# Two graph layers on one core: the second layer's input turned by VectorE from DRAM blocks, with features in another order

## The chip, the cores and the metric

The kernel runs on one core of a Trainium2 chip. Time is device microseconds of that core for one launch. Three runs of the kernel before gave a median of 1999.9 us (1999.46 to 2000.22).

## What is computed

x holds 128 graphs of 128 nodes with 256 features, adj 128 matrices of 128 x 128. Everything is 32-bit float. Two layers follow each other, each with a residual and a layer norm:

```
# layer 0
f_hom = adj @ ((x @ theta) * norm) * norm          # norm = (row sum of adj)^-0.5
f_het = x @ W_h
gate  = sigmoid(x @ W_t + b_t)
x1    = layernorm(x + elu(gate * f_hom + (1 - gate) * f_het))
# layer 1, on x1
h     = relu(bn1(conv1(x1)))                       # 1 tap, along the nodes
x_conv= relu(bn2(conv2(h)) + x1)                   # 17 taps along the nodes, 256 -> 256
s     = x1 @ w_se + b_se;  A = exp(-|s_n - s_m|^2) # node to node
x_nmp = A @ relu(x1 @ w_msg + b_msg)
out   = layernorm(x1 + GRU([x_conv, x_nmp], x1))
```

## The kernel before

The kernel has three stages, each with its own pools. P is 128 (partitions, nodes), D is 256 (features), NC = 2 halves of the features, J = 2 graphs in a pair, NP = 64 pairs.

**Stage A** (lines 541 to 643) runs over the pairs in rounds. A round of `a_round(t)` works on several pairs at once: TensorE projects pair t (`l0_project`, lines 343 and 348), VectorE and ScalarE finish layer 0 of pair t-1 (`l0_gate`, `l0_elu`, `l0_norm`), and layer 1 of pair t-2 and t-3 is begun: `l1_turn` makes x1 feature-major, `l1_front` multiplies it by conv1 (line 413), `l1_analyse` takes h to Fourier coefficients H (line 433). A product over features wants them on the partitions, while x1 comes out with nodes there. `transposed` (line 302) does this turn with four TensorE transposes (line 307) into a PSUM bank and one VectorE copy (line 311). x itself is turned in another way: `load` (line 117) reads it in 32-row blocks, so that the 32 x 32 block transpose of VectorE (line 317) completes the turn, without TensorE.

`l1_store` writes x1 (line 425) and its turned form x1T (line 426) to DRAM for stage C. `w_unit` (line 444) takes one group of conv2's taps to Fourier coefficients in every second round, at the end of the round (line 449, copied out by ScalarE at line 453 into four tiles), and `w_store` writes the four tiles in the next round (line 458). `v_unit` does the same for the eight leftover coefficients, in 19 of the other rounds (lines 480 and 484).

For rounds 3 to 63 the order is the one written in the code on TensorE, SyncE, VectorE and ScalarE; for rounds -1 to 2 it is on TensorE alone, and a scheduler orders the others. All DMAs of stage A but a few at the start and the end are issued by SyncE (SP), in the order: x1 store, x1T store, x, the x blocks of pair t+2 (four transfers), adj, then the tap store, the next tap load (four transfers), and the leftovers'. The program's DMA completion semaphores are eight, used in turn, so that the issue of a DMA waits until the one eight places before it has landed.

PSUM has eight banks in stage A, used in turn (`bank`, line 112). VectorE's order in a round is: turn of x1, three operations of `l0_gate`, a wait for ScalarE's exp, `l0_elu` with the layer norm's statistics, the gate's bias (line 355), the norm's shift (line 292, which waits for GpSimd), the shift of conv1 (line 417), the turn of x for the next pair, the row sum of adj, and the mix (line 374).

**The tail** (lines 614 to 642) finishes the last pairs and computes four groups' messages early, from x1T read back (`m_load`, line 499).

**Stage B** (lines 740 to 772) multiplies the coefficients H by those of the taps, 68 steps with 512 KB of taps each (line 743), while the gate weights are loaded on ScalarE's queue (`gate_weights`, line 704). **Stage C** reads x1T and x1 back, and computes the rest of layer 1.

Of the kernel before, what the change touches and what calls it, by code (L numbers as in the profile page):

```python
# [14 lines left out]
P = 128  # L15
# [19 lines left out]
def gnn_layers_kernel(ctx: ExitStack, tc: tile.TileContext, a: dict, out: bass.AP):  # L35
# [24 lines left out]
    x1_d = dtile([NP, P, J * D], "x1_d")  # L60
    x1T_d = dtile([NP, P, NC, J * P], "x1T_d")
    w_d = dtile([M // 2, P, 2, NC, D], "w_d")
# [9 lines left out]
    ones = const.tile([P, P], F32, tag="ones", name="ones")  # L72
    nc.gpsimd.memset(ones, 1.0)
# [37 lines left out]

    def bank(name):
        return ps.tile([P, 512], F32, tag="ps", name=name)
# [3 lines left out]
    def load(p):  # L117
        s = st[p] = {}

        xb = s["xb"] = io.tile([P, J * Q, 2 * K], F32, tag="xb", bufs=2, name=f"xb_{p}")  # L120
        for q in range(Q):
            nc.sync.dma_start(
                xb[q * K : (q + 1) * K],
                x[p * J : (p + 1) * J, :, 2 * K * q : 2 * K * (q + 1)].rearrange(
                    "b (r i) d -> i (b r) d", i=K
                ),
            )
        s["adjT"] = io.tile([P, J, P], F32, tag="adjT", bufs=3, name=f"adjT_{p}")
        nc.sync.dma_start(s["adjT"], adjT[:, p * J : (p + 1) * J, :])
# [14 lines left out]


    load(0)
    for j, name in enumerate(("L0_gnn_theta", "L0_gnn_W_h", "L0_gnn_W_t")):

        v = a[name].rearrange("(q c i) e -> c q i e", q=Q, c=NC)
        for c in range(NC):  # L150
            (nc.sync if j == 2 else nc.scalar).dma_start(w0[:, c, j * D : (j + 1) * D], v[c])
# [11 lines left out]
    vec = setup.tile([8 * NC, P], F32, tag="vec", name="vec")  # L163
    for i, q in enumerate("vmgb"):
        for k in range(2):
            r = (2 * i + k) * NC
            nc.scalar.dma_start(
                vec[r : r + NC], a[f"L1_gnn_bn{k + 1}_{q}"].rearrange("(c p) -> c p", p=P)
            )

    load(1)
    nc.sync.dma_start(conv1_w[:, :, 0:D], a["conv1_wT"].rearrange("(c p) e -> p c e", p=P))
    nc.sync.dma_start(conv1_w[:, :, D:], a["w_seT"].rearrange("(c p) e -> p c e", p=P))
# [61 lines left out]
    def batch_norms():  # L235
        n = 2 * NC
        tv = bank("vec_ps")
        nc.tensor.transpose(tv[:, 0 : 4 * n], vec, ident[0 : 4 * n, 0 : 4 * n])
        col = setup.tile([P, 4 * n], F32, tag="col", name="col")
        nc.vector.tensor_copy(col, tv[:, 0 : 4 * n])  # L240
        inv_sqrt(scale, col[:, 0:n], BN_EPS, n)
        nc.vector.tensor_mul(scale, scale, col[:, 2 * n : 3 * n])
        nc.vector.tensor_mul(shift, col[:, n : 2 * n], scale)
        nc.vector.tensor_sub(shift, col[:, 3 * n : 4 * n], shift)

        yield
        diag = setup.tile([P, n, P], F32, tag="diag", name="diag")
        for i, v in enumerate((scale, shift)):
            for c in range(NC):
                nc.vector.tensor_scalar(diag[:, NC * i + c, :], ident, v[:, c : c + 1], None, ALU.mult)  # L250
        tr = bank("row_ps")
        nc.tensor.matmul(tr, lhsT=ones, rhs=diag.rearrange("p a b -> p (a b)"), start=True, stop=True)
        nc.vector.tensor_copy(shift1, tr[:, D : 2 * D])
        for c in range(NC):
            nc.vector.tensor_mul(conv1_w[:, c, 0:D], conv1_w[:, c, 0:D], tr[:, 0:D])
# [46 lines left out]
    def transposed(src, dst, name):  # L302

        t = bank(f"{name}_ps")
        for c in range(NC):
            for j in range(J):
                nc.tensor.transpose(  # L307
                    t[:, (c * J + j) * P : (c * J + j + 1) * P],
                    src[:, j, c * P : (c + 1) * P], ident,
                )  # L310
        nc.vector.tensor_copy(dst.rearrange("p c n -> p (c n)"), t)


    def l0_turn(p):
        s = st[p]
        s["xT"] = wf.tile([P, NC, J * P], F32, tag="xT", name=f"xT_{p}")
        nc.vector.transpose(  # L317
            s["xT"].rearrange("p c (b i) -> p c b i", i=K),
            s["xb"].rearrange("p b (c i) -> p c b i", c=NC),
        )  # L320
        adj = bank(f"adj_ps_{p}")
        for j in range(J):
            nc.tensor.transpose(adj[:, nodes(j)], s["adjT"][:, j, :], ident)  # L323
        norm = s["norm"] = small.tile([P, J], F32, tag="norm", name=f"norm_{p}")
        nc.vector.reduce_sum(
            norm, adj[:, 0 : J * P].rearrange("p (j n) -> p j n", j=J), axis=mybir.AxisListType.X
        )
        inv_sqrt(norm, norm, DEG_EPS, J)
# [72 lines left out]

    def l1_turn(p):
        s = st[p]
        s["x1T"] = wk.tile([P, NC, J * P], F32, tag="x1T", bufs=2, name=f"x1T_{p}")
        transposed(s["x1"], s["x1T"], f"x1T_{p}")
# [17 lines left out]
    def l1_store(p, queue=nc.sync):  # L423
        s = st[p]
        queue.dma_start(x1_d[p], s["x1"].rearrange("p j e -> p (j e)"))
        queue.dma_start(x1T_d[p], s["x1T"])
# [17 lines left out]
    def w_unit(u):  # L444
        t = wt[u % NW].rearrange("p i o -> p (i o)")
        pq = [bank(f"w_ps_{u}_{r}") for r in range(4)]
        for r in range(4):
            k = slice(32 * r, 32 * r + TAPS)
            nc.tensor.matmul(pq[r], lhsT=T[k, 0:P], rhs=t[k, :], start=True, stop=True)  # L449
        wo = s_w[u] = []  # L450
        for r in range(4):
            o = taps.tile([P, 2, D], F32, tag="wo", bufs=4, name=f"w_o_{u}_{r}")
            nc.scalar.activation(o.rearrange("p i o -> p (i o)"), pq[r], AF.Copy)  # L453
            wo.append(o)

    def w_store(u):
        for r, o in enumerate(s_w.pop(u)):
            nc.sync.dma_start(
                w_d[0 : P // 2, r * QF + u].rearrange("k r c o -> k r (c o)"),
                o.rearrange("p c o -> p (c o)"),  # L460
            )
# [16 lines left out]
    def v_unit(v):  # L478
        pl = bank(f"wl_ps_{v}")
        nc.tensor.matmul(  # L480
            pl, lhsT=TL, rhs=vt.rearrange("p c o -> p (c o)"), start=True, stop=True
# [4 lines left out]
    def v_store(v):  # L486
# [3 lines left out]
        for r in range(2):  # L490
            nc.sync.dma_start(
                w_d[P // 2 : M // 2, f : f + n, r].rearrange("k f c o -> f k (c o)"),
# [6 lines left out]
    def m_load(i):  # L499
        t = io.tile([P, J, D], F32, tag=("xb", "x")[i // 2], bufs=2, name=f"mx1T_{i}")  # L500
        t = t.rearrange("p j d -> p (j d)")
# [39 lines left out]
    def a_round(t):  # L541
# [5 lines left out]
        def between():  # L547
            on(t - 1, l0_gate)
            on(t - 3, l1_analyse)
# [4 lines left out]
        on(t - 2, l1_turn)  # L554
        l0_project(t, between, beside) if t >= 0 else between()
        on(t - 1, l0_norm)
        if t == 0:
            next(norms)
            l0_turn(1)
            table(AT2, (node, lag))  # L560

            cos, sin = T[:, 2:M:2], T[:, 3:M:2]
            both = setup.tile([P, M // 2 - 1], F32, tag="both", name="both")
            nc.vector.tensor_sub(both, sin, cos)
            nc.vector.scalar_tensor_tensor(sin, sin, -1.0, cos, ALU.mult, ALU.subtract)
            nc.vector.tensor_copy(cos, both)
        on(t - 2, l1_front)
        on(t - 2, l1_store)
# [21 lines left out]
        if t != 0:  # L590
            on(t + 1, l0_turn)
        if t == 3:
            nc.scalar.dma_start(w_msg, a["w_msgT"].rearrange("(c p) e -> p c e", p=P))
# [13 lines left out]
    for t in range(-1, 3):  # L607
        with tc.manual_schedule(engines={E.PE}):
            a_round(t)

    with tc.manual_schedule(engines={E.PE, E.SP, E.DVE, E.Activation}):
        for t in range(3, NP):
            a_round(t)
        last = NP - 1
        l0_gate(last)
        w_unit(units[last])
        l1_turn(last - 1)
        l1_analyse(last - 2)
        l0_elu(last)
        early = [m_project(0, "gate")]  # L620
        l1_front(last - 1)
        m_load(2)
        l1_store(last - 1)
        w_store(units[last])
        m_load(3)
        l0_norm(last)
        early.append(m_project(1, "het"))
# [4 lines left out]
        l1_turn(last)  # L632
        early = [m_project(2, "gate")]
        l1_front(last)
        early[0][0]()
        l1_analyse(last - 1)
# [3 lines left out]
        l1_store(last, nc.scalar)  # L640
# [26 lines left out]
    def others():  # L667
# [36 lines left out]
        def gate_weights(t, name, lo_n, lo_rz):  # L704
            for at, width, base in ((lo_rz, D, 0), (lo_n, P, 2 * D)):
                for h in range(2):
                    nc.scalar.dma_start(
                        t[:, :, h, at : at + width],
                        a[name][:, base + h * width : base + (h + 1) * width].rearrange(
                            "(c p) e -> p c e", p=P  # L710
                        ),
# [3 lines left out]
        yield from gate_weights(w_ih, "w_ihT", D, 0)  # L715
        yield from gate_weights(w_hh, "w_hhT", 0, P)
# [23 lines left out]
    with tc.manual_schedule(engines={E.Activation, E.Pool}):  # L740
        for k in range(M // 2):
            w = wb.tile([P, 2, NC, D], F32, tag="w", name=f"wb_{k}")
            nc.sync.dma_start(w, w_d[k])
# [64 lines left out]
    def load_x1(g):  # L808
        s = st[g]
        if g in EARLY:  # L810
# [8 lines left out]
            s["x1"].rearrange("p (r j) e -> p r (j e)", j=J),  # L819
            x1_d[2 * g : 2 * g + 2].rearrange("r n e -> n r e"),  # L820
# [302 lines left out]
```

## Time and profile before

| from the page and the trace's answers | value |
|---|---|
| the profiled execution | 1999.04 us, of which the span is 1997.1 us |
| TensorE's granted clock, mean over the span | 0.995 |
| DMA packets | 245115, 263.64 MB, mean 132 GB/s |
| busy in 100 to 200 us (stage A): PE, DVE, ACT, POOL | 100.00, 81.46, 62.90, 17.75 us |
| stage A's DMA share, 100 to 600 us by stretches | 0.62 to 0.64 |
| stage B's DMA share, 720 to 800 us | 0.97, 347 GB/s |
| first turn of x1 (line 311) starts; last one | 34.6 us; 678.2 us |
| first matmul of stage B (line 748) | 686.2 us |

The span runs from the first to the last instruction of the program on the core; some 2 us of the execution lie around it. A row of an instruction group gives its count, the union of its busy times, the mean duration of one in ns, and the idle time of its engine just before it with what ended it. A matmul's duration includes the way through the array, which the next one overlaps; what one costs in a full stream is the distance from its start to the next one's start.

### The profile page before, as it was taken

What the parts mean: (1) busy time and instruction counts of PE and PEld (TensorE: products, weight loads), DVE (VectorE), ACT (ScalarE), POOL (GpSimd) and SP (SyncE); (2) the same over time, 40 slices, a digit from 0 to 9 for tenths busy, and PEclk for the clock granted to TensorE, in tenths of its full rate; (3) what the DMA queues carried; (4) which work ended last, traced back from release to release, by engine and by line L of the source; (5) the groups of instructions that cost most, each with busy time, mean ns of one, the idle gap of its engine ahead of it and who ended that gap; (6) DMA issues with size and microseconds to landing.
All of it is one profiled execution on the core that took longest, in us unless ns stands there. A gap on an engine that the chain in (4) does not pass through costs nothing.

```text
span 1997.1 us, 26580 instructions
## 1 busy us (share of the span) xinstructions
PE 1971.5 (99%) x8451; PEld 1348.2 (68%) x8451; DVE 1448.3 (73%) x2866; ACT 747.0 (37%) x1489; POOL 630.3 (32%) x855
## 2 busy tenths in 40 slices
PE   7999999999999999999999999999999999999997
PEld 5666666666666788876666666666666666666664
DVE  6888888888888664467777777767777776776766
ACT  3666666666666511122222222323222232222222
POOL 1111111111111255544243333424323342433331
PEclk8999999999999999999999999999999999999999
DMA  4666666656565689972212212221221221221100
GB/s 119 200 188 201 186 198 187 206 182 206 177 200 182 237 319 332 316 250 91 70 58 81 71 58 65 81 65 64 81 60 64 70 81 51 78 76 39 46 22 21
DMA packets 245115, 263.64 MB, mean 132 GB/s; under 512 B 86143, under 2 KB 179825, under 8 KB 244977
## 3 DMA queue, kind: packets, MB, share of 16 engines
q1 hardware_dynamic: 238641, 256.17, 40.2%
q10 hardware_dynamic: 6336, 5.78, 1.0%
q8 instruction: 69, 1.13, 0.2%
q14 instruction: 69, 0.57, 0.1%
HBM read 157.01 MB, written 104.86 MB: 131 GB/s over the span
## 4 chain that ended last, share of the span: by engine, by line
PE 95%; DVE 2%; DMA 1%; ACT 0%; issue 0%; POOL 0%; SPq 0%; POOLq 0%; DVEq 0%; ACTq 0%
PE g_ps L1007 43%; PE f_ps L343 11%; PE conv_ps L413 5%; PE y_ps L748 5%; PE gate_ps L348 5%; PE msg_ps L884 5%; PE coef_ps L433 3%; PE nmp_ps L940 3%; PE conv_ps L848 3%; PE z_ps L761 3%; PE mix_ps L369 3%; PE x1T_ps L307 2%; PE w_ps L449 2%; PE conv_ps L855 1%; PE wl_ps L480 1%; PE adj_ps L323 1%
## 5 line engine op out<-in xcount | busy, mean ns | idle before, releaser
L343 PE MATMUL f_ps<-w,xT 128*128 128x512 f32 x512 | 243.7, 599 | 0.2 <-DVE xT L317 0.2
L177 POOL TENSOR_SCALAR rstd_b<-mv_b 128x2 f32<-128x2 f32 (+1 forms) x65 | 12.5, 192 | 529.6 <-DVE mv_b L285 529.6
L966 ACT ACTIVATE o<-o 128x1024 f32<-128x1024 f32 (+1 forms) x65 | 67.9, 1044 | 268.4 <-DVE o L1043 263.9
L1007 PE MATMUL g_ps<-t_h,sh 128*128 128x384 f32 x384 | 156.9, 490 | 0.0
L1007 PE MATMUL g_ps<-t_m,sm 128*128 128x384 f32 x384 | 155.3, 486 | 0.0
L1007 PE MATMUL g_ps<-t_c,sc 128*128 128x384 f32 x384 | 155.2, 486 | 0.0
L294 ACT ACTIVATE y<-y,nb_b,rstd_b 128x256 f32<-128x256 f32 x128 | 70.0, 593 | 219.1 <-DVE nb_b L292 219.1
L348 PEld LDWEIGHTS gate_ps<-w,xT 128*128 128x128 f32 x512 | 97.3, 190 | 70.9 <-issue 60.9
L177 POOL TENSOR_SCALAR rstd_a<-mv_a 128x2 f32<-128x2 f32 x64 | 12.3, 192 | 392.2 <-DVE mv_a L285 379.8
L348 PE MATMUL gate_ps<-w,xT 128*128 128x256 f32 x512 | 132.0, 380 | 1.4 <-DMA w<-in_L_gnn_W_t 1.4
L343 PEld LDWEIGHTS f_ps<-w,xT 128*128 128x128 f32 x512 | 88.8, 192 | 63.0 <-issue 61.8
L1040 POOL TENSOR_TENSOR u<-u,p 128x512 f32<-128x512 f32 x63 | 79.8, 1266 | 162.4 <-DVE p L1024 162.4
L748 PE MATMUL y_ps<-wb,H 128*128 128x256 f32 x544 | 128.5, 379 | 0.8 <-issue 0.8
L413 PE MATMUL conv_ps<-conv_w,x1T 128*128 128x259 f32 x512 | 122.5, 381 | 0.0
L756 POOL TENSOR_TENSOR ws<-wb 128x512 f32<-128x512 f32 x67 | 92.7, 1384 | 89.7 <-PE z_ps L761 55.4
L352 ACT ACTIVATE hom<-f_ps,norm 128x256 f32<-128x256 f32 x128 | 60.6, 473 | 157.5 <-PE f_ps L343 153.0
L748 PEld LDWEIGHTS y_ps<-wb,H 128*128 128x128 f32 x544 | 103.2, 190 | 15.2 <-POOL ws L756 1.0
L884 PE MATMUL msg_ps<-w_msg,cx1T 128*128 128x256 f32 x480 | 108.7, 379 | 0.0
L1007 PEld LDWEIGHTS g_ps<-t_c,sc 128*128 128x128 f32 x384 | 73.0, 190 | 50.9
L1007 PEld LDWEIGHTS g_ps<-t_m,sm 128*128 128x128 f32 x384 | 73.0, 190 | 50.9
L413 PEld LDWEIGHTS conv_ps<-conv_w,x1T 128*128 128x128 f32 x512 | 97.1, 190 | 14.6 <-ACT w_o L453 0.2
L1007 PE MATMUL g_ps<-w_hhT_w,cx1T 128*128 128x384 f32 x256 | 105.1, 492 | 0.0
(218 smaller groups left out, 4433.7 us busy)
## 6 DMA issues: line engine op xcount, KB each, us to landing
wb<-w_d SPq DMA_DIRECT2D x68, 512.0 KB
w_d<-w_o SPq DMA_DIRECT2D x128, 256.0 KB
y_d<-yb SPq DMA_DIRECT2D x68, 256.0 KB
xb<-in_x SPq DMA_DIRECT2D x256, 64.0 KB
x<-in_x SPq DMA_DIRECT2D x64, 256.0 KB
cx1T<-x1T_d SPq DMA_DIRECT2D x64, 256.0 KB
yt<-y_d SPq DMA_DIRECT2D x32, 512.0 KB
cx<-x_d SPq DMA_DIRECT2D x32, 512.0 KB
```

The source lines that it names most:

```text
L294: nc.scalar.activation(dst[:, q, :], src[:, q, :], AF.Identity, bias=nb[:, q : q + 1], scale=rstd[:, q : q + 1],)
L343: nc.tensor.matmul(pf, lhsT=xT[:, c, nodes(j)], rhs=w0[:, c, 0 : 2 * D], start=(c == 0), stop=(c == NC - 1),)
L348: nc.tensor.matmul(pg[:, j * D : (j + 1) * D], lhsT=xT[:, c, nodes(j)], rhs=w0[:, c, 2 * D : 3 * D], start=(c == 0), stop=(c == NC - 1),)
L352: nc.scalar.activation(hom[:, j, :], pf[:, 0:D], AF.Copy, scale=norm[:, j : j + 1])
L369: nc.tensor.matmul(pm[:, j * D : (j + 1) * D], lhsT=adjT_[:, j, :], rhs=hom[:, j, :], start=True, stop=True,)
L413: nc.tensor.matmul(ph[:, 0 : D + CO], lhsT=s["x1T"][:, c, nodes(j)], rhs=conv1_w[:, c, :], start=(c == 0), stop=(c == NC - 1),)
L748: nc.tensor.matmul(py[:, blk, :], lhsT=coefs(blk if k == 0 else 2 * k + 1 - blk, c), rhs=w[:, blk, c, :], start=(c == 0), stop=(c == NC - 1),)
L756: nc.gpsimd.tensor_tensor(ws, w[:, 0], w[:, 1], ALU.add)
L884: nc.tensor.matmul(pm[:, j * D : (j + 1) * D], lhsT=x1T[:, c, nodes(q)], rhs=w_msg[:, c, :], start=(c == 0), stop=(c == NC - 1),)
L966: nc.scalar.activation(rz, rz, AF.Tanh, scale=0.5)
L1007: nc.tensor.matmul(pg[:, lo : lo + 3 * P], lhsT=s[f"f{kind}"][i][:, pr, :], rhs=factors[kind][i], start=(k == 0), stop=(k == 2), skip_grou ...
L1040: nc.gpsimd.tensor_tensor(u4, u2, p5, add)
```

## The change

x1 too is turned by VectorE. `l1_store` is split: x1 of pair t-2 is stored in round t as before, in the layout [pair, graph, node, feature], and `load_back` reads it in blocks of 32 nodes by 64 features into a new tile x1b (one buffer, four transfers, at the end of SyncE's round), and `l1_turn` transposes the blocks on VectorE in the next round. So conv1 and all behind it come one round later (pair t-3 in round t, `l1_analyse` t-4). The last two pairs still use TensorE (`l1_turn_now`).

A 32 x 32 block that is read in pieces of 64 features holds two features for each row of the turned block. They are now taken as feature 2p + c for partition p and half c, by a step of two elements in the reading of the transpose; w0, conv1, w_msg, the gates' weights and the taps' outputs follow that order. The taps' order is made where TensorE reads them (`w_unit`, `v_unit`).

The x blocks of two pairs are loaded together in each odd round (`load_blocks`), into one buffer of twice the size in place of two. A unit of taps is kept in one tile and stored in one transfer of 1 MB. The taps' array in DRAM has its coefficient index ahead of the partition, so that stage B reads two pieces of 2 KB for each partition in place of one of 4 KB. All rounds are in the written order on the four engines. The tables (`table`) move to the first round, and the tail is rearranged.

```diff
-    x1_d = dtile([NP, P, J * D], "x1_d")
+    x1_d = dtile([NP, J, P, D], "x1_d")
     x1T_d = dtile([NP, P, NC, J * P], "x1T_d")
-    w_d = dtile([M // 2, P, 2, NC, D], "w_d")
+    w_d = dtile([M // 2, 2, P, NC, D], "w_d")
...
     def load(p):
-        s = st[p] = {}
-
-        xb = s["xb"] = io.tile([P, J * Q, 2 * K], F32, tag="xb", bufs=2, name=f"xb_{p}")
+        s = st[p]
+        s["adjT"] = io.tile([P, J, P], F32, tag="adjT", bufs=3, name=f"adjT_{p}")
+        nc.sync.dma_start(s["adjT"], adjT[:, p * J : (p + 1) * J, :])
+
+    def in_blocks(dst, src):
+
         for q in range(Q):
             nc.sync.dma_start(
-                xb[q * K : (q + 1) * K],
-                x[p * J : (p + 1) * J, :, 2 * K * q : 2 * K * (q + 1)].rearrange(
-                    "b (r i) d -> i (b r) d", i=K
-                ),
+                dst[q * K : (q + 1) * K],
+                src[:, :, 2 * K * q : 2 * K * (q + 1)].rearrange("b (r i) d -> i (b r) d", i=K),
             )
-        s["adjT"] = io.tile([P, J, P], F32, tag="adjT", bufs=3, name=f"adjT_{p}")
-        nc.sync.dma_start(s["adjT"], adjT[:, p * J : (p + 1) * J, :])
+
+    def load_blocks(p, n):
+
+        if p % 2 == 0:
+            st["xb"] = io.tile([P, 2, J * Q, 2 * K], F32, tag="xb", bufs=1, name=f"xb_{p}")
+        t = st["xb"]
+        in_blocks(
+            t[:, p % 2 : p % 2 + n].rearrange("p h b d -> p (h b) d"), x[p * J : (p + n) * J]
+        )
+        for k in range(n):
+            st[p + k]["xb"] = t[:, p % 2 + k]
...
-        v = a[name].rearrange("(q c i) e -> c q i e", q=Q, c=NC)
-        for c in range(NC):
-            (nc.sync if j == 2 else nc.scalar).dma_start(w0[:, c, j * D : (j + 1) * D], v[c])
+        (nc.sync if j == 2 else nc.scalar).dma_start(
+            w0[:, :, j * D : (j + 1) * D], a[name].rearrange("(p c) e -> p c e", c=NC)
+        )
...
+    load_blocks(1, 1)
     load(1)
-    nc.sync.dma_start(conv1_w[:, :, 0:D], a["conv1_wT"].rearrange("(c p) e -> p c e", p=P))
-    nc.sync.dma_start(conv1_w[:, :, D:], a["w_seT"].rearrange("(c p) e -> p c e", p=P))
+    nc.sync.dma_start(conv1_w[:, :, 0:D], a["conv1_wT"].rearrange("(p c) e -> p c e", c=NC))
+    nc.sync.dma_start(conv1_w[:, :, D:], a["w_seT"].rearrange("(p c) e -> p c e", c=NC))
...
     def l0_turn(p):
         s = st[p]
         s["xT"] = wf.tile([P, NC, J * P], F32, tag="xT", name=f"xT_{p}")
-        nc.vector.transpose(
-            s["xT"].rearrange("p c (b i) -> p c b i", i=K),
-            s["xb"].rearrange("p b (c i) -> p c b i", c=NC),
-        )
+        turned(s["xT"], s["xb"].rearrange("p b (i c) -> p c b i", c=NC))
...
+    def x1T_tile(p):
+        t = st[p]["x1T"] = wk.tile([P, NC, J * P], F32, tag="x1T", bufs=2, name=f"x1T_{p}")
+        return t
+
+    def load_back(p):
+
+        t = st[p]["x1b"] = wk.tile([P, J * Q, 2 * K], F32, tag="x1b", name=f"x1b_{p}")
+        in_blocks(t, x1_d[p])
+
+    def turned(dst, src):
+
+        nc.vector.transpose(dst.rearrange("p c (b i) -> p c b i", i=K), src)
+
     def l1_turn(p):
-        s = st[p]
-        s["x1T"] = wk.tile([P, NC, J * P], F32, tag="x1T", bufs=2, name=f"x1T_{p}")
-        transposed(s["x1"], s["x1T"], f"x1T_{p}")
+        turned(x1T_tile(p), st[p]["x1b"].rearrange("p b (i c) -> p c b i", c=NC))
+
+    def l1_turn_now(p):
+
+        t = bank(f"x1T_{p}_ps")
+        for c in range(NC):
+            for j in range(J):
+                nc.tensor.transpose(
+                    t[:, (c * J + j) * P : (c * J + j + 1) * P],
+                    st[p]["x1"][:, j, c::NC], ident,
+                )
+        nc.vector.tensor_copy(x1T_tile(p).rearrange("p c n -> p (c n)"), t)
...
-    def l1_store(p, queue=nc.sync):
-        s = st[p]
-        queue.dma_start(x1_d[p], s["x1"].rearrange("p j e -> p (j e)"))
-        queue.dma_start(x1T_d[p], s["x1T"])
+    def x1_store(p, queue=nc.sync):
+        queue.dma_start(x1_d[p].rearrange("j n e -> n j e"), st[p]["x1"])
+
+    def x1T_store(p, queue=nc.sync):
+        queue.dma_start(x1T_d[p], st[p]["x1T"])
...
     def w_unit(u):
-        t = wt[u % NW].rearrange("p i o -> p (i o)")
+        t = wt[u % NW].rearrange("p i (o c) -> p i c o", c=NC)
         pq = [bank(f"w_ps_{u}_{r}") for r in range(4)]
         for r in range(4):
             k = slice(32 * r, 32 * r + TAPS)
             nc.tensor.matmul(pq[r], lhsT=T[k, 0:P], rhs=t[k, :], start=True, stop=True)
-        wo = s_w[u] = []
-        for r in range(4):
-            o = taps.tile([P, 2, D], F32, tag="wo", bufs=4, name=f"w_o_{u}_{r}")
-            nc.scalar.activation(o.rearrange("p i o -> p (i o)"), pq[r], AF.Copy)
-            wo.append(o)
+        wo = s_w[u] = taps.tile([P, Q, NC * D], F32, tag="wo", name=f"w_o_{u}")
+        for r in range(Q):
+            nc.scalar.activation(wo[:, r, :], pq[r], AF.Copy)
 
     def w_store(u):
-        for r, o in enumerate(s_w.pop(u)):
-            nc.sync.dma_start(
-                w_d[0 : P // 2, r * QF + u].rearrange("k r c o -> k r (c o)"),
-                o.rearrange("p c o -> p (c o)"),
-            )
+        nc.sync.dma_start(
+            w_d[0 : P // 2].rearrange("k s (r u) c o -> u (k s) r (c o)", r=Q)[u], s_w.pop(u)
+        )
...
+        if i == 0:
+            st["xb"] = io.tile([P, 2, J * D], F32, tag="xb", bufs=1, name="mx1T")
+        if i < 2:
+            t = st["xb"][:, i]
+        else:
+            t = io.tile([P, J, D], F32, tag="x", bufs=2, name=f"mx1T_{i}")
+            t = t.rearrange("p j d -> p (j d)")
...
-            on(t - 3, l1_analyse)
+            on(t - 4, l1_analyse)
...
-        on(t - 2, l1_turn)
+        on(t - 3, l1_turn)
...
-        on(t - 2, l1_front)
-        on(t - 2, l1_store)
+        on(t - 3, l1_front)
+        if t > 0 and t % 2 == 1 and t + 1 < NP:
+            load_blocks(t + 1, 2)
+        on(t - 2, x1_store)
+        on(t - 3, x1T_store)
...
+        on(t - 2, load_back)
+        on(t + 1, l0_turn)
+        if t == -1:
+            table(AT2, (node, lag))
+
+            cos, sin = T[:, 2:M:2], T[:, 3:M:2]
+            both = setup.tile([P, M // 2 - 1], F32, tag="both", name="both")
+            nc.vector.tensor_sub(both, sin, cos)
+            nc.vector.scalar_tensor_tensor(sin, sin, -1.0, cos, ALU.mult, ALU.subtract)
+            nc.vector.tensor_copy(cos, both)
+        if t == 0:
+            next(norms)
...
-    for t in range(-1, 3):
-        with tc.manual_schedule(engines={E.PE}):
-            a_round(t)
 
     with tc.manual_schedule(engines={E.PE, E.SP, E.DVE, E.Activation}):
-        for t in range(3, NP):
+        for t in range(-1, NP):
             a_round(t)
         last = NP - 1
+        l1_turn(last - 2)
         l0_gate(last)
         w_unit(units[last])
-        l1_turn(last - 1)
-        l1_analyse(last - 2)
+        l1_analyse(last - 3)
+        l1_front(last - 2)
+        x1_store(last - 1)
+        x1T_store(last - 2)
         l0_elu(last)
+        l1_turn_now(last - 1)
         early = [m_project(0, "gate")]
-        l1_front(last - 1)
         m_load(2)
-        l1_store(last - 1)
         w_store(units[last])
         m_load(3)
         l0_norm(last)
+        x1T_store(last - 1)
+        x1_store(last)
+        l1_analyse(last - 2)
+        l1_front(last - 1)
         early.append(m_project(1, "het"))
         for add, _ in early:
             add()
         for _, send in early:
             send()
...
+        yield from gate_weights(w_ih, "w_ihT", D, 0, 0, "(p c)")
+        yield from gate_weights(w_ih, "w_ihT", D, 0, D, "(c p)")
+        yield from gate_weights(w_hh, "w_hhT", 0, P, 0, "(p c)")
...
-            nc.sync.dma_start(w, w_d[k])
+            nc.sync.dma_start(w, w_d[k].rearrange("s p c o -> p s c o"))
```

## The prediction

> **What bounds the kernel now.** I read the busy shares and slices first, then two stretches, then the groups of stage A alone (100 to 640 us: 53 rounds, 10.19 us each), then one round in order of time, and last SyncE's issues beside the DMAs' landing marks.
>
> ```profile
> PE 1971.5 (99%) x8451; PEld 1348.2 (68%) x8451; DVE 1448.3 (73%) x2866; ACT 747.0 (37%) x1489; POOL 630.3 (32%) x855
> DMA  4666666656565689972212212221221221221100
> 100.00:200.00 100.00, 100.00 (x459) 69.01 (x458) 81.46 (x182) 62.90 (x147) 17.75 (x40) 1.00 0.63 195
> 720.00:800.00 80.00, 80.00 (x371) 70.17 (x370) 35.56 (x62) 11.87 (x31) 43.16 (x31) 1.00 0.97 347
> ```
>
> TensorE has no gap in stage A, at full clock. A busy TensorE need not be at its peak, but here its starts follow each other at the rate of the stream (line 348: 0.86 us for four in every round), so an operation taken from it is worth its distance between starts. The DMA engines are at 0.63 in A and 0.97 in B. VectorE at 81% looks free, but its order is fixed, so I look at what its waits are:
>
> ```profile
> L392 DVE SCALAR_TENSOR_TENSOR gate<-gate,x 128x512 f32<-128x512 f32 x52 | 36.0, 692 | 36.2 <-ACT gate L386 36.2
> L292 DVE SCALAR_TENSOR_TENSOR nb_a<-mv_a,rstd_a 128x2 f32<-128x2 f32 x53 | 8.5, 161 | 18.0 <-POOL rstd_a L178 18.0
> L311 DVE COPY x1T<-x1T_ps 128x512 f32<-128x512 f32 x53 | 36.2, 683 | 16.1 <-PE x1T_ps L307 16.1
> L417 DVE TENSOR_TENSOR h<-conv_ps,shift 128x256 f32<-128x256 f32 x106 | 43.6, 420 | 12.3 <-PE conv_ps L413 10.3
> L355 DVE TENSOR_TENSOR gate<-gate_ps,L_gnn_b_t_b 128x512 f32<-128x512 f32 x53 | 36.3, 685 | 8.6 <-PE gate_ps L348 7.9
> L317 DVE STREAM_TRANSPOSE xT<-xb 128x512 f32<-128x512 f32 x53 | 37.2, 702 | 0.2
> ```
>
> The last column counts: only 16.1 + 12.3 us (and the 7.9 in part) wait for TensorE and go when it gets ahead; 36.2 (exp) and 18.0 (GpSimd) stay. So VectorE's own round is (540 - 28.4)/53 = 9.65 us, 9.5 if the 7.9 goes too. It is the next bound, 0.54 us behind.
>
> **The change part by part.**
>
> *Transposes off TensorE.* The round:
>
> ```profile
> 403.15 0.66 PE L307 MATMUL x1T_ps<-ident,x 128*128 128x128 f32 x4
> 403.64 1.88 PE L343 MATMUL f_ps<-w,xT 128*128 128x512 f32 x4
> ...
> 413.42 0.60 PE L307 MATMUL x1T_ps<-ident,x 128*128 128x128 f32 x4
> 413.86 1.45 PE L343 MATMUL f_ps<-w,xT 128*128 128x512 f32 x3
> 403.84 0.69 DVE L311 COPY x1T<-x1T_ps 128x512 f32<-128x512 f32 x1 [0.61 <-PE x1T_ps L307]
> ```
>
> Start to start four transposes cost 0.49 or 0.44 us (53 rounds: mean 0.465), though the row's mean is 280 ns each; after a tap unit VectorE idles 0.61 us for them. The Trainium skill ("TensorE: Matmul & The Clock Gate", part 4, transpose mode) gives some 275 ns for one in a kernel's stream and says that the clock doesn't rise for it; by that, 62 pairs would bring 68 us, more than VectorE's slack lets through. The trace shows that 275 ns is one's duration, not its price. I take the spacing: 62 x 0.46 = **-28.5 us**. TensorE's round falls to 9.72, still above VectorE's 9.5 to 9.65: all of it comes through, if nothing else is late.
>
> *VectorE's copy becomes a transpose*: 702 for 683 ns, +0.02 x 62 = 1.2 us on an engine with that slack. Both transposes now read with a step of 8 bytes, which no transpose here does. Nearest row: line 684 copies 128 elements with steps of 32 bytes in 266 ns, as much as line 250 needs for 128 packed ones (272). So 0; upper end twice the streaming, 2 x 0.53 us a round, +60 us.
>
> *A step of two in TensorE's moving operand* (`w_unit`, `v_unit`): no row shows one. No gain can come of it; if the stream halves, 32 x 1.07 + 19 x 0.86 = +50 us (line 449 and line 480 start to start). The skill ("SBUF — State Buffer", Door 1) says that a 16-byte line wants two accesses to hold full rate; a step of two floats has just two. I take 0 and keep +50 for the range.
>
> *SyncE and the DMAs.* Issue costs from SyncE's rows: 0.45 us a block transfer, 0.56 a 256 KB tap store, 0.37 an x1 store. Per two rounds: load_back +8 x 0.5, joined x blocks -4 x 0.5, joined tap store -1.9: about even. The DMA engines get 256 KB more a pair: 1024 packets of 256 bytes, 18 ns each by the trace's packets, 1.15 us on each of 16 engines; x1 in 1 KB pieces, +0.1. Share: (6.4 + 1.25)/9.75 = 0.78. That is an average; the odd rounds of the first half get the double block load (2.3 us of engine time), the tap store (2.7 to 2.9), the tap load (0.8) and all else: 9.4 to 10.2 us of work in a round of 9.7.
>
> *The return of x1* is the new wait, and I follow one such round from VectorE's turn (0). The block loads wait for the turn of the buffer's second half, at -1.05; four issues, to +1.2. x1's store, which could go at -2.0 (before: 422.6, at 424.6 the turn), goes behind them, then x1T, x, adj: 2.8. Tap store 3.5, tap load 5.5, load_back from there. Landing takes 2.0 to 2.8 us after an issue in the trace. But the fourth piece is eight places behind the tap store and waits for its landing: the queue has 5.3 us of data before it, it ends near 8.1, lands near 8.5; the piece lands at **10.4 to 10.6**. VectorE wants it at 9.65, or 10.2 with a leftover copy: 0.3 to 0.9 late. Behind the waiting transpose stand all of VectorE's round, the x1T store on SyncE, and conv1 on TensorE. 16 such rounds x 0.6: **+9 us**. In other rounds load_back lands at 8.0 to 8.5, in time. In the second half the tap units fall in the odd rounds and their stores in the even ones: landing 9.8 against 9.65 to 10.2, about even.
>
> *The end of stage A.* `m_load(0)` takes the joined x buffer, so on SyncE it waits for the turn of pair 63, at about +8.6 of round 62, and the tap store and load_back(60) stand behind it: its landing comes at 13 to 15 instead of before 9.7. TensorE is some 1 us ahead: **+4 us**, once. One pair's conv1 and analysis, 1.75 + 0.93, moves into the tail: **+2.7**. At the start TensorE's idle time of 3.09 us before the first turn (33.15) goes: **-3.1**. w0 in three transfers with 16 engines each instead of four may take the gate's 1.4 us wait for W_t; the table now stands ahead of the gate on VectorE and may give it back: 0, +-2.
>
> *Stage B.* 68 loads in 2 KB pieces: 2 x 84 ns for 159 by the packets' medians, 8 pieces a step and engine: 68 x 0.07 = +4.9 us of DMA time. TensorE's 80.00 of 80 covers it, with the DMA share at 0.97: +1; without cover +5. Twelve gate weight issues for eight lie on ScalarE's queue, 12 of 80 us busy: 0. *Bias, norms, weights in the new order*: the same bytes: 0.
>
> Sum against the profiled execution: 1999.0 - 28.5 + 9 + 4 + 2.7 - 3.1 + 1 = **1984**. The median shown is 0.9 higher, which is less than I can claim.
>
> **The rivals.**
> - *Forecast*, 1984 (own range 1974 to 1993): chance 0.42.
> - *x1 is back in time*: the packets overlap better, or TensorE's lead takes the lateness: 1984 - 9 - 4 = 1971. For: before, everything landed 2.0 to 2.8 us after issue, no queue. Against: SyncE paced those; now the transfers are joined. 0.15.
> - *The gain is eaten*: about 0.8 us late per two rounds in both halves: 1995 to 2003. 0.12.
> - *The return becomes the bound*, on the slower side: one mechanism, the fourth piece of x1b behind the landing of the 1 MB tap store. It decides from 0.93 us of lateness per two rounds (2 x 0.465) in the mean. If 1 MB takes 1.5 us longer than I count, each tap round is 1.9 late: 31 x (1.9 - 0.93) = +30, plus the ends: 2033. If only the first half is so late, 2015. For: DMA share 1.03 in 410 to 412 us, when tap stores run alone. 0.18.
> - *Strided reading costs*: 1984 + 50 = 2034, or +60 on VectorE. 0.13.
>
> What a measurement here can tell from no change is 0.2%, 4 us. Faster 0.42 + 0.15 + 0.02 of the third: 0.59; same 0.10; slower 0.31. The range that leaves out no more than 2 in 10 reaches from the second rival's lower side, 1968, to 2018.
>
> **What will show it.** Right: no line 307 in the rounds, TensorE near 9.75 us a round; VectorE's x1T transpose at 0.70 us, idle before it for x1b by some 0.6 us in every second round up to about 330 us and hardly after; one long wait in round 62; DMA share 0.75 to 0.8. Wrong: transposes over 0.8 us or the tap matmuls over 1.2 us a unit (strides); x1b waits over 0.9 us (return); a stage B longer than its 178 us now, first y product at 686.2 to last z product at 864 (pieces). The forecast falls if TensorE shows gaps in every round.

## The result, and the profile after

The changed kernel takes 2032.97 us (median of 4, 2030.77 to 2034.06), the kernel before beside it 1999.68 (4 runs): a ratio of 1.0166, 95% interval 1.0148 to 1.0184. It is slower by 33 us, where 1984 was forecast. The profiled execution has a span of 2030.9 us.

First, where the 33 us lie. The marks are the starts of VectorE's row sum of adj (one in each round, counted from 0), of stage B's first product and of stage C's first transpose. Two of the experiments below stand beside: run 1, with the return of x1 moved ahead, and run 11, the last change made.

| us | before | after | run 1 | run 11 |
|---|---|---|---|---|
| start to row sum 0 | 12.2 | 8.7 | 8.0 | 9.0 |
| row sums 0 to 10 | 102.2 | 122.8 | 111.6 | 104.9 |
| row sums 10 to 32 | 226.2 | 235.7 | 219.1 | 219.0 |
| row sums 32 to 63 | 318.3 | 316.7 | 308.7 | 309.1 |
| row sum 63 to stage B | 27.4 | 37.5 | 33.7 | 30.1 |
| stage B | 178.3 | 176.8 | 177.8 | 178.0 |
| stage C | 1132.5 | 1132.7 | 1132.5 | 1132.5 |

Stages B and C are what they were. All of it is in stage A: 21 us in the first ten rounds, 9 in the rest of the first half, 10 in the tail, and a small gain in the second half.

From the page of the changed kernel: slices, and the rows (busy us, mean ns, idle before and its releaser) of TensorE's first product and of conv1.

```profile
PEclk8899999999999999999999999999999999999999
DMA  4567676777787589994222122222221221221100
L344 PE MATMUL f_ps<-w,xT 128*128 128x512 f32 x512 | 255.7, 623 | 23.2 <-DVE xT L414 22.2
L436 PE MATMUL conv_ps<-conv_w,x1T 128*128 128x259 f32 x512 | 125.6, 388 | 6.1 <-DVE x1T L414 5.6
```

TensorE, which had no gap in stage A, now waits for VectorE's turns (busy 213.40 of 220 us in 140 to 360). What VectorE waits for stands in its groups for 140 to 360 us (21 rounds), and in the list of waits (in total, times, longest) for 400 to 610 us:

```profile
L414 DVE STREAM_TRANSPOSE x1T<-x1b 128x512 f32<-128x512 f32 x21 | 14.9, 709 | 17.8 <-DMA x1b<-x_d 17.8
L414 DVE STREAM_TRANSPOSE xT<-xb 128x512 f32<-128x512 f32 x21 | 14.8, 702 | 0.0
```

```profile
DVE x1T L414 <- DMA x1b<-x_d: 9.6, 13, 1.8
```

The transposes cost what was forecast, 0.71 and 0.70 us. The return of x1 is the wait: 0.85 us a round in the first half, 0.47 in the second. In the first half 15.2 of the 17.8 us stand in the ten tap rounds (rounds with a tap store and tap loads ahead of the return): 0 to 2.7 us in one, 1.5 in the mean. One of the long ones in order of time (start, duration, engine):

```profile
228.07 1.91 SPq L126 DMA_DIRECT2D xb<-in_x  x4
229.05 0.70 DVE L414 STREAM_TRANSPOSE x1T<-x1b 128x512 f32<-128x512 f32 x1
230.08 0.44 SPq L447 DMA_DIRECT2D x_d<-x  x1
231.61 0.74 SPq L121 DMA_DIRECT2D adjT<-in_adjT  x1
232.44 0.56 SPq L479 DMA_DIRECT2D w_d<-w_o  x1
233.09 3.49 SPq L154 DMA_DIRECT2D wt<-in_conv_wT  x4
236.64 1.90 SPq L126 DMA_DIRECT2D x1b<-x_d  x4
241.45 0.71 DVE L414 STREAM_TRANSPOSE x1T<-x1b 128x512 f32<-128x512 f32 x1 [2.33 <-DMA x1b<-x_d]
```

Counted from the turn at 229.05, as the prediction counts: x1's store goes out at 1.0, the tap store at 3.4, the tap loads from 4.0 to 7.5, the four pieces of x1b from 7.6 to 9.5. The last lands at 12.3 (241.37, the last of its 16 landing marks; the other 15 were in by 240.06); VectorE stood ready at 10.1. The prediction had the tap loads done at 5.5 and the landing at 10.4 to 10.6.

### The profile page after: what moved, and what is told of

It reads as the page before. It is cut to its first block, busy times and chain, and to the rows that moved or that the text cites. A ratio compares the mean times of both kernels' runs of the same rounds, so it can differ in the third digit from the quotient of the medians.

```text
span 2030.9 us, 25948 instructions
## 1 busy us (share of the span) xinstructions
PE 1974.4 (97%) x8203; PEld 1333.4 (66%) x8203; DVE 1442.8 (71%) x2866; ACT 740.9 (36%) x1489; POOL 632.6 (31%) x855
## 4 chain that ended last, share of the span: by engine, by line
PE 79%; DVE 8%; DMA 6%; issue 2%; SPq 2%; ACT 1%; POOL 1%; DVEq 0%; POOLq 0%; ACTq 0%
PE g_ps L1037 42%; PE f_ps L344 7%; PE y_ps L779 5%; PE msg_ps L914 5%; DMA x1b<-x_d 3%; PE nmp_ps L970 3%; PE conv_ps L878 3%; PE gate_ps L349 3%; PE conv_ps L436 3%; PE z_ps L792 3%; DMA w_d<-w_o 2%; PE coef_ps L457 2%; PE mix_ps L370 1%; SPq L126 1%; PE conv_ps L885 1%
## 5 line engine op out<-in xcount | busy, mean ns | idle before, releaser
L344 PE MATMUL f_ps<-w,xT 128*128 128x512 f32 x512 | 255.7, 623 | 23.2 <-DVE xT L414 22.2
L192 POOL TENSOR_SCALAR rstd_a<-mv_a 128x2 f32<-128x2 f32 x64 | 12.3, 193 | 439.0 <-DVE mv_a L300 433.2
L1037 PEld LDWEIGHTS g_ps<-t_h,sh 128*128 128x128 f32 x384 | 71.6, 190 | 49.0 <-issue 1.4
```

Source lines behind the costliest of these rows:

```text
L344: nc.tensor.matmul(pf, lhsT=xT[:, c, nodes(j)], rhs=w0[:, c, 0 : 2 * D], start=(c == 0), stop=(c == NC - 1),)
L1037: nc.tensor.matmul(pg[:, lo : lo + 3 * P], lhsT=s[f"f{kind}"][i][:, pr, :], rhs=factors[kind][i], start=(k == 0), stop=(k == 2), skip_grou ...
```

## The experiments

The times below are medians, with the ratio to the kernel before, measured beside each, and its 95% interval.

**1. The return ahead of the tap transfers.**

```diff
+        on(t - 2, load_back)
         if t - 1 in units:
             w_store(units[t - 1])
...
-        on(t - 2, load_back)
         on(t + 1, l0_turn)
```

> The changed kernel with one edit: on SyncE's queue the four transfers that bring x1 back stand ahead of the tap store, tap load and leftover-tap transfers of their round, instead of behind them. Theory 'queue order' (the pieces are issued last of the round, behind a tap store and four tap loads that take SyncE 4.1 us, so they land 14.0 us after the xT turn where VectorE wants them at 10.4): VectorE's waits for x1b between 140 and 360 us fall from 17.8 to under 4 us, the rounds there from 10.5 to about 9.8 us, whole time 1985 to 2003. Rival 'too many bytes' (the DMA engines at 0.71 to 0.79 cannot bring 256 KB more a pair in time wherever they are issued): waits stay over 12 us, or turn up at the tap matmuls or the xb turn; 2022 or more.

Measured: 1993.36 us, 0.9974 (0.9963 to 0.9985). One line moved, the same bytes, 39.6 us less than the changed kernel. The return now stands ahead of the tap store, the tap loads and the store and load of the leftovers (`v_store`, `v_load`). Of VectorE's waits for x1b, 0.2 us are left between 140 and 360 us. The same kind of round:

```profile
230.95 0.43 SPq L447 DMA_DIRECT2D x_d<-x  x1
232.48 0.55 SPq L121 DMA_DIRECT2D adjT<-in_adjT  x1
234.71 1.81 SPq L126 DMA_DIRECT2D x1b<-x_d  x4
236.56 0.57 SPq L479 DMA_DIRECT2D w_d<-w_o  x1
237.23 3.29 SPq L154 DMA_DIRECT2D wt<-in_conv_wT  x4
240.57 0.69 DVE L414 STREAM_TRANSPOSE x1T<-x1b 128x512 f32<-128x512 f32 x1
```

SyncE stands still from 233.03 to 234.71 because x1's store must land before it can be read; even so the pieces are back at 238.11, before VectorE wants them. The rival of too many bytes falls: TensorE is busy again (209.56 of 210 us in 400 to 610), with the DMA share at 0.76 to 0.81.

**2. No return; 3. a return that nobody waits for.** In the first, every pair's x1 is transposed by TensorE, as before; the second is the same, but the 248 transfers are still issued.

```diff
-        on(t - 3, l1_turn)
+        on(t - 3, l1_turn_now)
...
-        l1_turn(last - 2)
+        l1_turn_now(last - 2)
...
-        on(t - 2, load_back)      # in run 2 only
```

> The changed kernel without the return: every pair's x1 is transposed by TensorE and copied out by VectorE, as only the last two pairs are in it; x1 is not read back. All else (feature order, joined x blocks, joined tap store, one round more of lag, start, end) stays. Theory 'the return is the loss': rounds go back to the 10.2 us that TensorE's transposes set before, first ten rounds under 113 us for 122.8, time 2003 to 2015 (1999 plus the longer tail of some 7 us, less 3 at the start). Rival 'the joined transfers or the start are the loss': 2022 or more, with gaps on TensorE as now.

> The run without the return (TensorE transposes every pair), but with the 248 transfers that read x1 back still issued at their places; nobody reads what they bring. It prices the traffic and SyncE's issues alone, with no wait on them. Theory 'the wait is the price': within 5 us of the run without them. Rival 'too many bytes': 10 us or more above it, TensorE waiting for x blocks or tap weights.

Measured: 2007.89 us (1.0046, 1.0031 to 1.0061) and 2008.46 (1.0049, 1.0034 to 1.0064). The two windows of 400 to 610 us (busy PE, PEld, DVE, ACT, POOL; clock; DMA share; GB/s), first without the transfers, then with them:

```profile
400.00:610.00 210.00, 210.00 (x948) 144.62 (x947) 168.71 (x371) 130.68 (x305) 35.61 (x80) 1.00 0.62 190
```

```profile
400.00:610.00 210.00, 210.00 (x948) 144.61 (x947) 168.71 (x370) 130.67 (x305) 35.62 (x80) 1.00 0.75 217
```

Of the DMA engines' time 0.13 more is used, and the time is 0.6 us longer, less than either range. Here the traffic is nearly free; the wait on it is not. The 8 us above the kernel before are what the rest of the change costs when TensorE still does the turns. Nearly half of it lies in these turns: reading with a step of two, four transposes take 0.52 us start to start, where they took 0.465.

**4. The tap store in four transfers.**

```diff
-        nc.sync.dma_start(
-            w_d[0 : P // 2].rearrange("k s (r u) c o -> u (k s) r (c o)", r=Q)[u], s_w.pop(u)
-        )
+        wo = s_w.pop(u)
+        d = w_d[0 : P // 2].rearrange("k s (r u) c o -> u (k s) r (c o)", r=Q)[u]
+        for r in range(Q):
+            nc.sync.dma_start(d[:, r], wo[:, r, :])
```

> The changed kernel with the 1 MB tap store issued as four transfers of 256 KB from the same tile; nothing else differs. Theory of the prediction (the fourth x1b piece stands eight places behind the tap store and waits for its landing, 5.5 us after its issue): the store's own wait shortens to 2.6 us, waits for x1b shrink by 0.5 us or more a tap round, 2010 to 2025. Rival 'place on the queue' (what counts is how much SyncE issues ahead): three more issues put the pieces up to 1.5 us later, unless the tap loads issue faster without a 1 MB store ahead of them; 2028 to 2050.

Measured: 2045.87 us, 1.0236 (1.0221 to 1.0251), 13 us slower than the changed kernel. The prediction's reason for the lateness, a fourth piece that waits for the landing of a 1 MB store, is not what binds: here it goes out right behind the third in each of the ten tap rounds from 140 to 360 us, and lands as late as in the changed kernel (11.7 us after the turn in the mean, in both).

```profile
233.20 2.29 SPq L482 DMA_DIRECT2D w_d<-w_o  x4
235.58 2.44 SPq L154 DMA_DIRECT2D wt<-in_conv_wT  x4
238.07 2.89 SPq L126 DMA_DIRECT2D x1b<-x_d  x4
```

SyncE needs 4.82 us here for store and loads (233.20 to 238.02), 4.14 in the changed kernel; the tap loads alone go faster, 2.44 for 3.49. VectorE's waits for x1b grow from 9.6 to 14.1 us in 400 to 610, and hardly (17.8 to 18.3) in 140 to 360. Over all of stage A they grow from 55 to 65 us, which is about the 10.5 us between the spans of the two profiled executions (2041.4 and 2030.9).

**5. The tap loads behind the return, the store still ahead.**

```diff
             w_store(units[t - 1])
-            if units[t - 1] + NW < NU:
-                w_load(units[t - 1] + NW)
...
         on(t - 2, load_back)
+        if t - 1 in units and units[t - 1] + NW < NU:
+            w_load(units[t - 1] + NW)
```

> The changed kernel with the four tap loads moved behind the return on SyncE's queue; the 1 MB tap store stays ahead of it. Theory 'SyncE's issue time' (behind the store the four tap loads take 3.5 us to issue, and the pieces of x1 start only then): the pieces go out 3.5 us earlier; their bytes still queue behind the store's, which land 5.5 us after its issue, so they come some 2 us earlier than now; waits for x1b between 140 and 360 us fall from 17.8 to 4 to 10 us, time 2005 to 2020. Rival 'the store's bytes' (the pieces cannot land before the store has, whenever they are issued, and that alone makes them late): waits stay at 15 us or more, 2026 to 2036.

Measured: 2012.48 us, 1.0070 (1.0055 to 1.0085); waits for x1b 7.0 us in 140 to 360, 8.1 in 400 to 610. The waits and the time fall where the theory had them. The round shows something that was not expected:

```profile
221.99 0.55 SPq L479 DMA_DIRECT2D w_d<-w_o  x1
222.65 3.61 SPq L126 DMA_DIRECT2D x1b<-x_d  x4
226.37 1.81 SPq L154 DMA_DIRECT2D wt<-in_conv_wT  x4
```

Now the pieces of x1 take 3.61 us to issue (1.90 in the changed kernel), and the tap loads 1.81 (3.49). The slow issues belong to whatever stands behind the 1 MB store, not to the tap loads. The store lands at 227.64, 5.65 us after its issue, and the pieces at 227.95 to 228.65, just behind it, the last 2.9 us after its issue. The Trainium skill ("DMA: Bandwidth & Descriptors", HWDGE ordering) says that each DMA engine takes the descriptors of a queue in order; these landings agree with it. So the tap loads ahead of the return cost 20.5 us (2032.97 - 2012.48).

The other 19.1 (to 1993.36) are not the tap store's alone. Run 1 also moves the return ahead of the store and load of the leftovers, and run 5 leaves them ahead. Of run 5's waits for x1b from 140 to 610 us, 1.9 us stand in the 22 rounds with a tap store, 12.9 in the 15 rounds with the leftovers' transfers. A round of that kind in the changed kernel:

```profile
405.19 0.40 SPq L493 DMA_DIRECT2D vt<-in_conv_wT  x1
405.69 1.97 SPq L126 DMA_DIRECT2D x1b<-x_d  x4
410.94 0.71 DVE L414 STREAM_TRANSPOSE x1T<-x1b 128x512 f32<-128x512 f32 x1 [0.66 <-DMA x1b<-x_d]
```

The pieces are issued early, but they land at 410.29 to 410.82, behind the leftovers' load ahead of them (410.11, 4.9 us after its issue). How the 19.1 us divide between tap store and leftovers, no run shows.

**6. The start scheduled as before.** In the changed kernel, rounds -1 to 2 again have a written order on TensorE alone.

```diff
+    for t in range(-1, 3):
+        with tc.manual_schedule(engines={E.PE}):
+            a_round(t)
     with tc.manual_schedule(engines={E.PE, E.SP, E.DVE, E.Activation}):
-        for t in range(-1, NP):
+        for t in range(3, NP):
```

> The changed kernel with the start scheduled as before: in rounds -1 to 2 only TensorE's order is fixed, VectorE, ScalarE and SyncE are left to the scheduler. It prices the fixed order at the start. Theory 'fixed order costs the start' (TensorE waits 5.6 us for the diagonals of the norm weights and 1.1 us for a copy, both behind a pair's work on VectorE, and its clock halves for 10.2 us after it): 6 to 12 us faster than the changed kernel, 2021 to 2027. Rival 'the start is late for x1 too': the gaps only move to the first returns of x1, within 4 us of 2033.

Measured: 2028.10 us, 1.0145 (1.0128 to 1.0162): 4.9 us faster, between the two ranges (6 to 12 us, and within 4 us), so that neither is confirmed. TensorE's wait for the norm weights (5.6 us) is gone, and a wait of 7.15 us for xT of pair 2 stands in its place. The written order at the start is a small part of the loss.

**7. The early x1T behind the return in the last two rounds**, on top of run 1.

```diff
         else:
+            on(t - 2, load_back)
             m_load(t + 2 - NP)
...
-        on(t - 2, load_back)
+        if t + 2 < NP:
+            on(t - 2, load_back)
```

> The run with the return ahead of the tap transfers, and in the last two rounds also ahead of the load of the early x1T, which waits for the turn of pair 63 because it takes the joined x buffer. Theory (that wait holds back x1b of pair 60 by 8 us on SyncE, VectorE idles 2.7 us for it and TensorE 2.6 us for h behind it): 3 to 6 us faster than that run, 1987 to 1991. Rival (the end is set by the longer order of the tail, not by that wait): within 2 us of 1993.

Measured: 1991.17 us, 0.9962 (0.9947 to 0.9977): 2.2 us less than run 1, below the expected 3 to 6 and hardly above the rival's 2. In the trace the stretch from row sum 63 to stage B shrinks by 3.6 us (33.7 to 30.1); the first ten rounds of this execution ended 1.5 us later.

**8. The norm weights a round later; 10. the table behind pair 1's turn; 9. idle products in TensorE's waits.** All three are on top of run 7; in run 8 two memsets of these tables stay in round 1.

```diff
-        if t == 1:                                  # run 8
+        if t == 2:
             next(norms, None)
             way_back()
...
-        if t == -1:                                 # run 10
+        if t == 0:
             table(AT2, (node, lag))
...
+        if t == 0:                                  # run 9: 28 here, 42 in round 1
+            keep_warm(28)
```

> As the run before this one, and with the norm weights' product and the tables of the way back moved from round 1 to round 2, ahead of the mix, so that pair 1's mix does not stand behind them on TensorE. If the 5.6 us wait at the start and the halved clock after it are a loss of their own: 5 to 10 us faster than the run before this one, 1978 to 1985. If VectorE's chain sets the start anyway (it has 8.8 us of table and 6 us of norms to do in its first rounds): within 3 us of it.

> The run with the return ahead of the tap transfers and of the early x1T, with 28 and 42 products of 128x128 that nobody reads put into TensorE's two waits of the start (3.9 us before pair 1's projection, 4.7 us before the norm weights' product). Theory 'the clock takes a second toll' (each of these waits is followed by 6.8 and 10.2 us at half clock, in which TensorE does 8.5 us less work): with the gaps filled the clock stays full to 60 us, and 4 to 8 us go, 1983 to 1987. Rival 'VectorE's chain sets the start' (whatever TensorE loses there it would have waited for VectorE): the clock is full but the time within 2 us of 1991.

> The same run (return ahead of the tap transfers and of the early x1T) with the cosine table's 8.8 us on VectorE put behind the gate of pair 0 and the turn of pair 1 instead of ahead of them, where the kernel before has it. Theory 'the table's place': TensorE's 3.9 us wait for xT of pair 1 goes and 2 to 5 us with it. Rival 'VectorE has too much to do in its first three rounds, wherever the table stands': within 2 us of 1991, the wait turning up at the next xT.

Measured: 1992.22 us (0.9967, 0.9954 to 0.9980), 1994.77 (0.9982, 0.9973 to 0.9990) and 1993.88 (0.9977, 0.9969 to 0.9986). None is faster than run 7. In run 8 the wait moves to round 2 (4.67 us for the same diagonals at 41.01), in run 10 it grows to 14.99 us at 36.81: VectorE has the work, and TensorE waits for it somewhere. Run 9 was inconclusive: its products took 6.41 and 9.54 us where the waits are 3.9 and 4.7.

**11. The message weights early.** In run 7 one long wait of the start was left, and SyncE's and ScalarE's issues show where it comes from:

```profile
55.55 0.33 ACTq L623 DMA_DIRECT2D w_msg<-in_w_msgT  x1
55.93 0.45 ACTq L624 DMA_DIRECT2D b_msg<-in_L_gnn_b_msg  x1
58.20 2.08 SPq L126 DMA_DIRECT2D x1b<-x_d  x4
61.79 0.71 DVE L414 STREAM_TRANSPOSE x1T<-x1b 128x512 f32<-128x512 f32 x1 [4.57 <-DMA x1b<-x_d]
```

The weight lands at 58.19 and the bias at 58.95; the first piece of x1b goes out at 58.20, the second at 58.97. They stand eight places behind, and ScalarE's transfers count in that turn. In the changed kernel the same two hold the tap store (issued at 58.06, the weight landed at 58.00), behind it stand the tap loads and the return, and VectorE waits 8.84 us.

```diff
-        if t == 3:
+        if t == 0:
             nc.scalar.dma_start(w_msg, a["w_msgT"].rearrange("(p c) e -> p c e", c=NC))
```

> The run with the return ahead of the tap transfers and of the early x1T, with ScalarE's two transfers of the message weight and bias issued in round 0 instead of round 3. In that run the first two pieces of x1b of pair 1 go out at 58.20 and 58.97 us, just after these two have landed (58.19 and 58.95), and VectorE waits 4.57 us for them. Theory 'semaphores in turn' (SyncE's pieces wait for the transfers eight places earlier, ScalarE's among them): the wait goes and 3 to 5 us with it, 1986 to 1988.5. Rival (the start is held by other waits): within 2 us of 1991.

Measured: 1984.77 us, 0.9930 (0.9917 to 0.9944): 6.4 us less than run 7, more than expected. The piece goes out at 51.77, and the turn at 56.37 no longer waits:

```profile
51.77 1.93 SPq L126 DMA_DIRECT2D x1b<-x_d  x4
53.80 0.62 SPq L479 DMA_DIRECT2D w_d<-w_o  x1
56.37 0.70 DVE L414 STREAM_TRANSPOSE x1T<-x1b 128x512 f32<-128x512 f32 x1
```

**12. The same with 17 and 21 idle products.**

> The run with the message weights early, and with 17 and 21 idle products in TensorE's two waits of the start; in the run that tried 28 and 42 they took 6.4 and 9.5 us, twice what the waits are, since one of them is two passes. If the halved clock after the waits costs time of its own: 3 to 7 us faster than the run without them, 1980 to 1985. If VectorE's chain sets the start: within 2 us of it.

Measured: 1984.50 us, 0.9929 (0.9917 to 0.9942), the same as without them. The windows of 10 to 120 us, first run 11, then run 12:

```profile
10.00:120.00 110.00, 98.62 (x383) 62.91 (x381) 87.58 (x207) 57.60 (x133) 18.78 (x41) 0.94 0.67 187
```

```profile
10.00:120.00 110.00, 103.10 (x458) 69.77 (x457) 86.81 (x207) 57.42 (x133) 18.23 (x41) 0.98 0.66 187
```

The clock rises from 0.94 to 0.98 and nothing comes of it. With runs 8 and 10 this says that VectorE's chain sets the time at the start, and that the halved clock takes only what TensorE would have waited.

Runs 11 and 12 beat both kernels, by 0.7% against the kernel before. They keep the whole change: three places on the two queues are different from it (run 12 has the idle products besides).

## Why the prediction was wrong

**The step that failed** is the return of x1, and in it the term "tap store 3.5, tap load 5.5, load_back from there", with waits of 0.6 us in 16 rounds, +9 us. The four tap loads behind the 1 MB store take 3.5 us of SyncE, not 2. In the mean of the ten tap rounds from 140 to 360 us, the first piece goes out 7.5 us after the turn (5.5 counted) and the fourth, which decides, at 9.1 (8.5 counted, since it was to wait until then). It lands at 11.7, where 10.4 to 10.6 was counted, and the wait is 1.5 us for 0.6. Some 0.6 us of the mean landing come from four of the ten rounds, the one shown among them, in which the last of a piece's 16 landing marks comes 1.2 to 2.2 us after the other 15. Why, no run shows.

Beneath it lies "joined tap store -1.9": I took three issues off SyncE at their price and left the price of the issues behind them. Before, four stores and four loads took 4.6 us; joined, 4.1. The joining saved 0.5 us.

```profile
408.37 2.51 SPq L458 DMA_DIRECT2D w_d<-w_o  x4
410.98 2.02 SPq L143 DMA_DIRECT2D wt<-in_conv_wT  x4
```

A second term was put at nothing: "In other rounds load_back lands at 8.0 to 8.5, in time". The leftovers' store and load were not counted. Where they stand ahead, the pieces land at 9.3 to 9.9 us in 140 to 360 us, and VectorE, ready at 9.4 to 9.5, waits 0.33 us in the mean. Run 1 prices the place of the return behind all these transfers: 39.6 us, of which the prediction had 9.

**Its reason was wrong too.** The wait for the landing of the store, eight places ahead, was to hold the fourth piece. In seven of the ten tap rounds it goes out less than 0.1 us after the issue of the third is done (in the one shown at 238.09, SyncE being free at 238.04 and the store landed at 237.94); in three it is held, by 0.1 to 0.5 us. Run 4 took that hold away and was slower.

**The second half** was called "about even"; it has waits of 0.47 us a round, and its time fell by some 1.5 us. They stand more in the rounds with leftovers (5.4 us from 400 to 610) than in those with a tap store (4.4), which the prediction had in mind. The step that made the return's own rival decide at 0.93 us per two rounds was of the right kind: the first half, with 1.7 us of waits per two rounds (2 x 0.85), lost against before, the second, with 0.94, came out near even.

**The start**: the 3.1 us forecast were TensorE's wait before the first turn, at 33 us. That wait went, but waits of 3.9 us (for xT of pair 1) and 5.6 us (for the norm weights) came in its place. The 3.5 us gained before row sum 0 are another thing: the first x blocks are turned at 6.87 us instead of 10.68. The message weights' two transfers and the eight-place turn were in the text of the kernel and in the trace of before, where TensorE had no gap behind them; where a return waits behind them they cost 6.4 us (run 11). The prediction followed only a round of the middle.

**The tail**: the stall behind the early x1T was forecast at 4 us; VectorE's wait was 5.6 us. In run 1 it is 2.7, and taking that out gained 2.2. The +2.7 for one pair more in the tail is what is left in run 11 (30.1 for 27.4).

**The transposes**: the size was off. With the return in time (run 1), the distance between row sums from 140 to 610 us falls from 10.29 to 9.97 us, 0.32 and not 0.46 a round, 62 x 0.32 = 20 us and not 28.5. The 0.465 went, but start to start other products of TensorE take more in the mean round: f_ps 0.06 us, the tap and leftovers' units 0.05, mix 0.04. In the units most of it is there in run 2 too, which shares their step of two. f_ps is the same in each tap round, 0.53 us for the first product behind the unit where 0.43 stood; whether the rest is waiting or a fixed cost is not traced. The mean hides one thing more: six of 46 rounds have neither taps nor leftovers, took 9.36 us before and take 9.31 in run 1, so there was hardly anything to gain in them. The round of 9.72 was also a misreading: 540 us hold 52.5 rounds, not 53, so the rounds before were 10.28 long.

**Right**: the bytes fit (run 3); VectorE's transposes take 0.70 to 0.71 us with their step of two, as without; the tap unit's step costs 0.04 us (1.07 to 1.11, start to start); 2 KB pieces cost stage B nothing (178.3 to 176.8). The time came out at the edge of the rival "the return becomes the bound" (2015 to 2033), which names the right place with the wrong cause. That run 11's 1984.8 equals the forecast is chance: 20 us of gain for 28.5, less tail and start.

The parts, in the order in which the runs took them out of the changed kernel's 2033.0: tap loads ahead of the return 20.5, tap store and leftovers' transfers ahead of it 19.1, early x1T in the tail 2.2, message weights 6.4. In another order each may weigh differently. They are differences of medians taken at different times, and the kernel before, measured beside each, took 1998.2 to 1999.7 us.

## What to carry to other kernels

When an engine begins to wait for a round trip through memory, the trip's place on the issuing queue is part of its price: put it ahead of everything that nobody waits for, even if the queue must then stand still for the store to land. Count issues from a row in which they stand behind the same neighbour, and look for one-off transfers, of other engines too, in the same turn of semaphores. A kernel that keeps its transfers and drops only the wait (run 3) separates traffic from waiting in one run.

## What was not expected of the hardware

An issue behind a 1 MB store is slow, whatever it is. In run 5 the second and third piece of x1 took 1.13 and 1.26 us, in the changed kernel the third tap load 1.18, where most such issues take 0.4 to 0.6; the stretch ends 3 to 4 us after the store's issue. It is not tied to one large transfer: in run 4, behind four stores of 256 KB, one piece of x1 took 1.44 us, and in the kernel before one tap load in such a round took 1.27. Why, no run shows.

TensorE's clock halved for 3.4, 6.8 or 10.2 us after some of its waits of 0.9 to 5.6 us, while other waits of 1.0 and one of 2.0 us passed without it: 44 us of stage A in the changed kernel, 10 before. It read like a second toll on each gap; run 12 shows that at the start, where another engine sets the time, it cost nothing.
